# Priorities and PSUM banks in the tail of a four-layer convolution kernel: the last group's work against the third group's

## The chip, the cores and the metric

The kernel runs on one core of one Trainium2 chip. The metric is the device time of one execution in microseconds (us): the median of three runs. A profiled execution, taken apart from these, gives the trace; its times are counted from the start of its span. The engines are named as the profile has them: PE (matmuls), PEld (its weight loads), DVE (vector), ACT (activation), POOL, and SP (here only a queue that issues DMAs).

## The reference

The input x has shape (16, 32, 128, 128): 16 images of 32 channels. Four layers follow each other, each of the form x = x + layer(group_norm(x)) with 16 groups of two channels. The functions and the weights' names are the reference's, abridged:

```python
x = x + L0(gn(x), W2, b2, W1, b1)       # a recurrent layer that scans the diagonals of the image
x = x + L1(gn(x), weight)               # a 3x3 layer of sums of absolute differences, quantised
x = x + L2(gn(x), weights1)             # 2D Hartley transform, 32x32 low modes mixed, transformed back
x = x + L3(gn(x), conv1 .. conv7, deconv1 .. deconv3)

def L3(x):
    y = concatenate([norm(corr(x, op)) for op in five_edge_operators], axis=1)
    y = maxpool2(conv3x3(y, conv1))     # 160 -> 32 channels
    y = maxpool2(conv3x3(y, conv2))
    y = maxpool2(conv3x3(y, conv3))
    y = conv3x3(y, conv4)
    y = conv3x3(deconv2x2(y, deconv1), conv5)
    y = conv3x3(deconv2x2(y, deconv2), conv6)
    y = conv3x3(deconv2x2(y, deconv3), conv7)
    return x * y
```

The edge operators are linear and their norms need only a mean and a variance, so an edge operator, its norm and conv1 are together one 5x5 convolution of the image with weights that depend on the image's statistics.

## The kernel before, in words

The 16 images are worked as four groups of four images. Layer 0 runs first, on its own. Then `rest` (L498) does layers 1 to 3. Its class `Differences` makes layer 1 for all images with DVE (L760) and ACT (L757), summed on PE (L647). Its class `After` makes layers 2 and 3 of one group after the other. `After.work` is a Python generator: each step records a few instructions and yields how long they take or what is to be waited for. A `Weave` holds such a generator, a time `now` and a list of steps that are put off until later.

While layer 1 is being recorded, `Differences.run` draws steps of groups 0 to 2 from the first weave between its own, and `keep_order` (L471) then fixes that order on every engine. What is left of the third group (its last 5x5 chunk and all that follows) and the whole last group are recorded by `drain` (L455): of the two weaves it always takes the one whose `now` is smaller. When one of them has ended, the other gets `alone` = True.

This last part, the tail, has no order fixed by hand. The scheduler that lays out the program takes, among the instructions that its own estimate holds for ready, the one with the smallest priority number. The number is `tc.cur_priority` at the time of recording and counts up with each instruction, so that in the kernel before the order of recording decides. A queue, once laid out, is worked in its order on each engine, and SP's DMA issues are such a queue too.

The steps of one group that matter, with the lines that the profile shows:

- Layer 2, `forward`: images are loaded (`xh`, L1056), scaled by `scaling` (L1155 to L1170, with the matmuls L786, L795 and L1165), and transformed on PE by `first` (L1107), `turned` (L1122) and `second` (L1079), with DVE in between (L1111, L1067, L1070, L1083). The modes go to DRAM (`xm`, L1089) and come back (L1183); DVE adds mirrored modes (L1190, L1197). `mixing` multiplies with the weights `mix` (loads L1205, matmuls L1218), and the result goes through DRAM (L1242, L1273).
- Layer 2, `back`: the inverse transform in two steps. L1292 makes `o1` in two halves of four accumulators each, emptied by DVE (L1304). L1342 makes 16 pieces of two accumulators each; `take_out` adds a piece to the image on DVE (L1317) and takes its statistics (L1320). L1359, L786, L795 and small DVE steps up to L1361 make mean and scale.
- Layer 3, first part: ACT normalises the image (L1382), `statistics` sums products of shifted rows into four accumulators `gram` on PE (L1488), DVE reduces them with tables (L1557), and the weights of the 5x5 layer are made (L1625, L1627).
- Layer 3, `conv1` (the 5x5 layer): edge sums first (L1844), copied by L1856, then eight chunks of 16 rows. A chunk is 25 taps of 16 matmuls (L1871) into four accumulators of 128x512 fp32; edges are mended by L1888. At its end DVE adds the cut columns (L1905) and pools (L1764), and ACT or DVE adds the bias (L1789, L1786).
- Layer 3, the rest: conv2, conv3 and conv4 (L1661), then three upsampling steps of `Composed.round` (L908, with bias matmuls L934), the third of which is `last`, eight rounds of 128 L908 and 32 L934; each is multiplied into the residual by DVE (L1993), finished by ACT (L1958) and stored (L1967).

The last group is worked by `end`, a shallow copy of `after` with larger buffers, its image kept whole in SBUF (`whole`), and a PSUM pool of its own. The pool `b_ps` (`bg`) has four banks and serves groups 0 to 2; `c_ps` has the other four and serves the last group. `acc` (L995) hands out one bank: before the change, while `alone` is true every other four of the last group's accumulators come from `bg`, which is its `spare`; otherwise all come from its own pool. An accumulator can only be given out when what read the bank's previous content is done.

Of the kernel before, what the change touches and what calls it, by code (L numbers as in the profile page):

```python
# [350 lines left out]
class Weave:  # L351
# [59 lines left out]
    def step(self):  # L411
# [3 lines left out]
        if v is None:  # L415
            return None
        if v is SUMMED:
            wait = self.lag()
# [33 lines left out]
                self.pe = start + us * CLOCK  # L452


def drain(*weaves):  # L455

    live = list(weaves)
    for w in live:
        w.draining, w.stretch = True, 1.5
    while live:  # L460
        w = min(live, key=lambda w: w.now)
        us = w.step()
        w.now = max(w.now + (us or 0.0), w.until)
        w.due(float("inf") if us is None else w.now)
        if us is None:
            live.remove(w)
            for w in live:
                w.alone, w.stretch = True, 1.0


def keep_order(nc, tc, start):  # L471

    last = {}
    for i in nc.cur_bb.bb.instructions[start:]:
        if i.engine in last:
            tc.add_manual_dep(
                i,
                last[i.engine].name,
                mybir.DependencyInfo(mybir.DependencyClass.NoSync, mybir.DependencyReason.DATA),
                reason="order",  # L480
            )
        last[i.engine] = i
# [5 lines left out]
LATE, ACT_SPARE = 1.5, 1.5  # L488
SLACK, CLOCK = 1.0, 1.0
SUMMED = ("summed",)  # L490


def rest(nc, tc, cst, sel16, bias, m1, r1, a, d, out):


    with ExitStack() as ctx:
        sm = ctx.enter_context(tc.tile_pool(name="s1_sm", bufs=1))
        stat = sm.tile([128, B, 8, 6], F32, name="stat2")  # L498
        with tc.tile_pool(name="s1_ps0", bufs=2, space=PSUM) as ps:
            first = Differences(nc, sm, ps, cst, sel16, m1, r1, a["adder_w"], d, stat)  # L500
        bg = ctx.enter_context(tc.tile_pool(name="b_ps", bufs=4, space=PSUM))
        after = After(nc, tc, "left", sm, bg, cst, bias, a, d, stat, out)
        weave = after.weave = Weave(after.work(range(NG - 1)))
        start = len(nc.cur_bb.bb.instructions)
        with ExitStack() as front:
            first.run(tc, front, weave)
        keep_order(nc, tc, start)

        end = copy.copy(after)
        end.side, end.ps = "right", ctx.enter_context(tc.tile_pool(name="c_ps", bufs=4, space=PSUM))  # L510
        end.spare, end.whole = bg, True

        end.buffers = {"t_x": 8, "xm": 8, "xw": 4, "t_w": 6, "t_r": 8, "frames": 3, "gm": 5, "e_v": 6, "l_x": 4}
        end.weave = Weave(end.work([NG - 1]))
        end.weave.now = end.weave.base = weave.now
        end.weave.finished = B - 1
        drain(weave, end.weave)


class Differences:  # L520
# [259 lines left out]
def normalised(nc, pool, ps, weave, mv, n, avg, eps, out):  # L780
# [5 lines left out]
    nc.tensor.matmul(p[:, :n], avg, mean, start=True, stop=True)  # L786
    yield SUMMED
    nc.vector.tensor_copy(out[:, 0], p[:, :n])
# [6 lines left out]
    nc.tensor.matmul(p[:, :n], avg, v, start=True, stop=True)  # L795
    yield SUMMED
    nc.vector.tensor_copy(v, p[:, :n])
# [35 lines left out]
class Composed:  # L833
# [10 lines left out]
    def compose(self, pool, ps):  # L844
# [5 lines left out]
        for par in range(4):  # L850
            for tap in range(4):
# [6 lines left out]
                for i, (q, k) in enumerate(terms):  # L858
# [8 lines left out]
                    yield 0.4  # L867
        yield SUMMED
        t = pool.tile([128, 25, 32], F32, name="co_t")
# [9 lines left out]
        nc.vector.tensor_reduce(t[:, 24], w3.rearrange("p t o -> p o t"), AX.X, ALU.add)  # L879
        yield SUMMED  # L880
        nc.sync.dma_start(self.store, t.rearrange("p t o -> p (t o)"))
        p = ps.tile([128, 512], F32, name="acc")
        for j in range(4):
            nc.tensor.matmul(p[32 * j : 32 * j + 32, :1], t[:32, 24], self.bd[:32], start=True, stop=True)
        yield SUMMED
        nc.vector.tensor_add(self.bias, p[:, :1], self.b3)
# [76 lines left out]
class After:  # L963


    def __init__(self, nc, tc, side, sm, ps, cst, bias, a, d, stat, out):
        self.nc, self.tc, self.side, self.ps, self.cst, self.bias = nc, tc, side, ps, cst, bias
        self.a, self.d, self.stat, self.out = a, d, stat, out
        self.spare, self.banks, self.whole = None, 0, False
        self.sm, self.scales = sm, {}  # L970
        self.buffers = {"t_x": 4, "xm": 3, "xw": 2, "t_w": 3, "t_r": 4, "frames": 2, "gm": 3, "e_v": 3, "l_x": 2}
        store = [d["up"][i] for i in range(3)]
        self.up5 = Composed(nc, sm, a, "deconv1", "conv5", bias[:, 7:8], bias[:, 4:5], store[0])
        self.up6 = Composed(nc, sm, a, "deconv2", "conv6", bias[:, 8:9], bias[:, 5:6], store[1])
        self.up7 = Composed(nc, sm, a, "deconv3", "conv7", bias[:, 9:10], bias[:, 6:7], store[2])
# [19 lines left out]
    def acc(self):  # L995

        self.banks += 1
        ps = self.spare if self.weave.alone and self.banks // 4 % 2 else self.ps
        return ps.tile([128, 512], F32, name="acc")

    def prepare(self):
# [812 lines left out]
    def conv1(self, g, pool, frames, y1, sides, wf, b1):  # L1814

        nc, tc, cst, weave = self.nc, self.tc, self.cst, self.weave

        def tap_of(n, i):

            at, const = PART_AT[n]  # L1820
            size = PARTS[n][4] * PARTS[n][5]
            return wf[:, const if i == size else at + i, :]

        _, _, _, again, _, window = frames
# [33 lines left out]

        spreads = []
        for ch in range(8):  # L1860
            xp = window(ch)

            acc = [self.acc() for _ in range(4)]
            apart, at = (32, 4 * ch) if self.whole else (8, 0)
            edge = {0: ("t", 0, 0, 1), 7: ("b", 3, 3 * W, at + 3 * apart + 5)}.get(ch)
            for tap in range(25):
                kh, kw = tap // 5, tap % 5
                for j in range(4):
                    for blk in range(4):
                        rows = slice(32 * blk, 32 * blk + 32)  # L1870
                        nc.tensor.matmul(  # L1871
                            acc[blk][32 * j : 32 * j + 32, :],
                            tap_of("all", tap)[rows],
                            xp[rows, at + apart * j + kh : at + apart * j + kh + 4, kw : kw + W],
                            start=tap == 0,
                            stop=tap == 24,
                        )
                if edge and tap == 23:
                    n, j, first, row = edge
                    for part, col, wide in ((n, 0, 5), (n + "l", 1, 2), (n + "r", W + 1, 2)):  # L1880
                        width = W if wide == 5 else 1
                        o = first + (W - 1 if part == n + "r" else 0)
                        for cut_tap in range(2 * wide + 1):
                            for blk in range(4):
                                rows = slice(32 * blk, 32 * blk + 32)
                                c = col + cut_tap % wide
                                src = xp[rows, row + cut_tap // wide, c : c + width]
                                nc.tensor.matmul(  # L1888
                                    acc[blk][32 * j : 32 * j + 32, o : o + width],
                                    tap_of(part, cut_tap)[rows],  # L1890
                                    cst["ones"][rows, :width] if cut_tap == 2 * wide else src,
                                    start=False,
                                    stop=False,
                                    skip_group_check=True,
                                )
                            yield 0.1
                yield 1.06
            yield SUMMED
            if ch + ahead < 8:
                again(ch + ahead)  # L1900
            out = []
            for blk in range(4):
                sides_of = acc[blk].rearrange("p (r w) -> p r w", w=W)[:, :, :: W - 1]
                both = cut[:, blk, :, 4 * ch : 4 * ch + 4].rearrange("p s r -> p r s")
                nc.vector.tensor_tensor(sides_of, sides_of, both, ALU.add)  # L1905
                weave.dve += 0.17
                out.append(self.pooled(pool, acc[blk], 4, W))

            def spread(ch=ch, out=out):
                for blk in range(4):  # L1910
                    self.evict(
                        y1[:, blk, 1 + 2 * ch : 3 + 2 * ch, 1:65], out[blk], b1[:, blk : blk + 1], blk, nc.scalar
                    )
                if ch in (0, 7):
                    self.neighbours(y1, 16, ch == 7, ch == 0)

            spreads.append(weave.later(5.0, spread))
            yield -2.0
# [248 lines left out]
```

## Time and profile before

| what | us |
|---|---|
| median of 3 runs | 6466.08 |
| lowest and highest run | 6465.73, 6471.06 |
| profiled execution, its own time | 6473.52 |
| its span | 6471.7 |
| PE, DVE, ACT busy over the span | 5326.5, 5455.2, 5276.5 |
| last layer-1 instruction on DVE (L630) ends | 5632.5 |
| third group's last 5x5 chunk ends on PE | 5677.5 |
| last group's mixing (L1218) starts, ends | 5753.1, 5787.4 |
| its first and last take-out (L1317, L1320) | 5869.5, 5921.7 |
| its Gram matmuls (L1488) end | 6033.2 |
| its edge sums (L1844) start | 6067.2 |
| its 5x5 layer (L1871) starts, ends | 6087.3, 6302.5 |

The page shows busy time in 40 slices of 161.8 us each; the tail begins in slice 35. The stage views of the profile give, for each stretch of time, the busy time of each engine with the count of records, the mean granted PE clock (1.00 is full), and the share of the DMA engines. A timeline row is a start, a duration, an engine, a line, an operation, tiles, shapes and a count; in brackets stand the idle time ahead of it and what ended it. The chain of waits goes back from the last instruction to what released it at each step; "issue" is time in which PE waited for nothing that the profile shows.

### The profile page before, as it was taken

The numbers are of one execution on the slowest core, as the hardware profiler recorded it, in microseconds if no ns is written. First come the engines' busy times: TensorE is split into PE (matmuls) and PEld (weight loads), VectorE is DVE, ScalarE is ACT, GpSimd is POOL, SyncE is SP. The second block draws the span as 40 slices with busy tenths as digits, with TensorE's granted clock in tenths as the row PEclk, the third lists the DMA queues.
The fourth block names the chain that finished last, engine by engine and source line by source line (L and its number), as shares of the span: only waits on it lengthen the run. The fifth ranks groups of instructions, "written<-read, shape, count | busy, mean of one in ns | idle before, by whom it ended". The sixth has DMA issues, their size and how long they took to land.

```text
span 6471.7 us, 275922 instructions
## 1 busy us (share of the span) xinstructions
PE 5326.5 (82%) x130160; PEld 2805.8 (43%) x130160; DVE 5455.2 (84%) x6528; ACT 5276.5 (82%) x2779; POOL 58.7 (1%) x67
## 2 busy tenths in 40 slices
PE   3689577788877879998877879998888699977696
PEld 3576233344434433334443433334344333345594
DVE  7899899999999989999999889999999899834212
ACT  3899799999999989999999879999999899702001
POOL 0000000000000000000000000000000000000000
PEclk9999899999999989999999989999999899977898
DMA  7643313121154633222455532323455522344102
GB/s 313 222 178 125 87 48 84 48 57 45 32 138 124 204 117 88 64 72 73 142 147 150 168 93 58 97 51 102 129 144 179 162 58 63 97 131 137 33 4 65
DMA packets 363701, 700.94 MB, mean 108 GB/s; under 512 B 67972, under 2 KB 216452, under 8 KB 351684
## 3 DMA queue, kind: packets, MB, share of 16 engines
q1 hardware_dynamic: 355092, 648.86, 33.6%
q0 software_dynamic: 7040, 33.80, 1.6%
q8 instruction: 1018, 16.68, 1.1%
q14 instruction: 119, 0.97, 0.1%
q10 hardware_dynamic: 432, 0.64, 0.0%
HBM read 500.46 MB, written 182.69 MB: 106 GB/s over the span
## 4 chain that ended last, share of the span: by engine, by line
PE 26%; issue 11%; DVE 8%; ACT 3%; DMA 2%; SPq 0%; POOL 0%; DVEq 0%; ACTq 0%; POOLq 0%
PE acc L1871 10%; PE acc L647 9%; DVE d_dve L760 4%; PE acc L908 3%; ACT d_act L757 2%; PE acc L1661 1%; PE acc L1488 1%; PE acc L1292 1%; DMA xm_d<-xm 0%; PE acc L1218 0%; PE acc L662 0%; DVE pooled L1764 0%; PE acc L934 0%; DMA v<-fold_d 0%; PE acc L1844 0%
## 5 line engine op out<-in xcount | busy, mean ns | idle before, releaser
L757 ACT ACTIVATE d_act<-q,neg 128x8192 f16<-128x8192 f16 (+1 forms) x630 | 4463.6, 7152 | 215.9 <-PE acc L647 197.4
L760 DVE TENSOR_SCALAR d_dve<-q,qw 128x8192 f16<-128x8192 f16 (+1 forms) x1674 | 3868.3, 2360 | 215.3 <-PE acc L647 193.1
L647 PE MATMUL acc<-d_dve,sel 128*32 128x512 f16 x26784 | 1850.6, 395 | 409.4 <-DVE d_dve L760 305.6
L647 PEld LDWEIGHTS <-sel 128*32 128x32 f16 x36864 | 983.9, 99 | 1934.0 <-issue 1265.0
L647 PE MATMUL acc<-d_act,sel 128*32 128x512 f16 x10080 | 708.5, 401 | 147.9 <-ACT d_act L757 140.8
L1871 PE MATMUL acc<-xp,wf 32*32 32x512 f32 x19200 | 725.4, 607 | 23.0 <-issue 21.5
L677 PE MATMUL acc<-q,zero 128*32 128x512 f16 x8396 | 576.7, 390 | 7.1 <-issue 7.0
L223 PE MATMUL pg<-h,wb 64*64 64x20 f32 (+15 forms) x8192 | 341.3, 304 | 61.6 <-DVE h L251 34.8
L908 PE MATMUL acc<-y,u_conv 32*32 32x256 f32 x10752 | 318.4, 435 | 60.7 <-issue 45.1
L237 ACT ACTIVATE gt<-pg,bias 128x20 f32<-128x20 f32 (+15 forms) x1024 | 331.5, 383 | 41.6 <-PE pg L223 39.7
L1871 PEld LDWEIGHTS acc<-xp,wf 32*32 32x32 f32 x19200 | 222.4, 103 | 329.2 <-issue 297.9
L677 PEld LDWEIGHTS <-zero 128*32 128x32 f16 x8396 | 243.6, 99 | 228.1 <-issue 40.6
L1789 ACT ACTIVATE y<-pooled,b 128x128 f32<-128x128 f32 x112 | 39.5, 395 | 368.3 <-DVE pooled L1764 235.0
L223 PEld LDWEIGHTS pg<-h,wb 64*64 64x64 f32 x8192 | 251.4, 150 | 136.4 <-DVE h L251 81.5
L908 PEld LDWEIGHTS acc<-y,u_conv 32*32 32x32 f32 x10752 | 157.0, 110 | 164.3 <-issue 122.8
L1871 PE MATMUL acc<-image,wf 32*32 32x512 f32 x6400 | 207.8, 605 | 0.1
L223 PE MATMUL pg<-xn,wb 64*64 64x2 f32 (+63 forms) x4096 | 184.5, 290 | 25.9 <-issue 17.9
L1871 PEld LDWEIGHTS acc<-image,wf 32*32 32x32 f32 x6400 | 184.8, 103 | 20.3 <-issue 4.6
L1488 PE MATMUL acc<-xp 32*64 32x204 f32 (+2 forms) x6432 | 174.2, 338 | 15.8 <-issue 15.8
L1905 DVE TENSOR_TENSOR acc<-acc,cut 128x8 f32<-128x8 f32 x128 | 19.4, 166 | 193.4 <-PE acc L1871 193.1
L1661 PE MATMUL acc<-y,w_conv 32*32 32x512 f32 (+2 forms) x4608 | 144.3, 481 | 30.3 <-issue 18.0
L662 PE MATMUL acc<-q,sel 32*32 32x512 f16 x4608 | 158.4, 393 | 4.0 <-issue 4.0
(242 smaller groups left out, 3725.9 us busy)
## 6 DMA issues: line engine op xcount, KB each, us to landing
q<-q_d SPq DMA_DIRECT2D x128, 536.2 KB, 10.2
xp<-xn_d SPq DMA_DIRECT2D x24, 2112.0 KB, 9.1
x_in<-in_x_dram SPq DMA_DIRECT2D x16, 2048.0 KB, 14.7
xn<-in_xs_dram SPq DMA_DIRECT2D x64, 512.0 KB, 7.0
res<-in_x_dram SPq DMA_DIRECT2D x64, 512.0 KB, 8.9
x_d<-res SPq DMA_DIRECT2D x64, 512.0 KB, 4.6
xq<-x_d SPq DMA_DIRECT2D x256, 128.0 KB, 4.4
xr<-x_d SPq DMA_DIRECT2D x256, 128.0 KB, 4.3
```

Source lines behind the costliest of these rows:

```text
L223: nc.tensor.matmul(bank[c][q][64 * pair : 64 * pair + 64, :, :width], wb[half, 4 * kind + KIND[q]].rearrange("p b o -> p (b o)"), v[half], ...
L237: nc.scalar.activation(gt[:, q, :, :n], bank[c][q][:, :, :n], AF.Tanh if q == G else AF.Sigmoid, bias=bias[:, KIND[q] : KIND[q] + 1],)
L647: self.nc.tensor.matmul(acc[k][32 * j : 32 * j + 32, :], self.sel16[:, i // 9, :], d[:, row : row + 4, c : c + W], start=first, stop=last,)
L662: self.nc.tensor.matmul(acc[k][32 * j : 32 * j + 32, :], self.sel16[rows, 8, :], q[rows, row : row + 4, kw : kw + W], start=False, stop=False,
L677: self.nc.tensor.matmul(acc[k][32 * j : 32 * j + 32, :], self.zero, q[:, :4, :W], start=False, stop=False)
L757: nc.scalar.activation(dst, src, AF.Relu, bias=self.neg[:, i : i + 1])
L760: nc.vector.tensor_scalar(dst, src, self.qw[:, i : i + 1], 0.0, ALU.subtract, ALU.max)
L908: nc.tensor.matmul(acc[blk][32 * j : 32 * j + 32, o : o + rows * n], t[part, 4 * par + tap, :], own[:, top : top + rows, left : left + n], ...
L1292: nc.tensor.matmul(pa[blk][32 * r : 32 * r + 32, 32 * o : 32 * o + 32], zi[part, 16 * oh + o, :], cst["cas_t"][part, 32 * r : 32 * r + 32] ...
L1488: nc.tensor.matmul(gram[blk][j : j + width, at : at + n], xp[part, l, 2 + j : 2 + j + width], xp[part, rows, j : j + width + 4], start=sta ...
L1661: nc.tensor.matmul(acc[blk][32 * j : 32 * j + 32, : rows * n], wc[name][part, tap, :], pick(part, blk, j)[:, tap // 3 : tap // 3 + rows, t ...
L1871: nc.tensor.matmul(acc[blk][32 * j : 32 * j + 32, :], tap_of("all", tap)[rows], xp[rows, at + apart * j + kh : at + apart * j + kh + 4, kw ...
```

## The change

`drain` gets the tile context. It gives each of the two weaves a count of priorities of its own: the third group's starts at the current number plus 2,000,000, the last group's at plus 1,000,000. Before each step it sets `tc.cur_priority` to that weave's number and keeps it afterwards. Which weave records next is decided as before, so the instructions and their order of recording are the same. The bank rule in `acc` changes: `spare` is used when `self.late` is true, in place of when the weave is alone; `late` is set False in `__init__`, and at each chunk of `conv1` to whether the chunk is the fifth or a later one. `alone` still decides how DVE and ACT share `evict` and `spread`. Below `BEHIND` all line numbers grow by four.

```diff
-def drain(*weaves):
+def drain(tc, *weaves):
 
     live = list(weaves)
+    turn = {w: tc.cur_priority + BEHIND * (len(live) - k) for k, w in enumerate(live)}
     for w in live:
         w.draining, w.stretch = True, 1.5
     while live:
         w = min(live, key=lambda w: w.now)
+        tc.cur_priority = turn[w]
         us = w.step()
         w.now = max(w.now + (us or 0.0), w.until)
         w.due(float("inf") if us is None else w.now)
+        turn[w] = tc.cur_priority
         if us is None:
             live.remove(w)
...
+BEHIND = 1000000
...
-        drain(weave, end.weave)
+        drain(tc, weave, end.weave)
...
-        self.spare, self.banks, self.whole = None, 0, False
+        self.spare, self.banks, self.whole, self.late = None, 0, False, False
...
-        ps = self.spare if self.weave.alone and self.banks // 4 % 2 else self.ps
+        ps = self.spare if self.spare and self.late and self.banks // 4 % 2 else self.ps
...
-            xp = window(ch)
+            xp, self.late = window(ch), ch >= 4
```

## Prediction

> **What bounds the kernel now.** I read the page's slices first: until slice 35 DVE, ACT and PE are full; from about 5629 us of the span on, only the tail (third group's end and the whole last group) runs. I then took that tail stage by stage (busy time by stage), because the change touches nothing earlier.
>
> ```profile
> core 0: us, PE busy (x) PEld busy (x) DVE busy (x) ACT busy (x) POOL busy (x), PEclk, DMA share, GB/s
> 5753.00:5788.00 35.00, 20.91 (x1247) 17.36 (x1245) 8.98 (x19) 0.00 (x0) 0.00 (x0) 0.55 0.20 65
> 5788.00:5870.00 82.00, 50.52 (x2339) 35.80 (x2317) 17.08 (x36) 2.55 (x4) 0.00 (x0) 0.62 0.63 177
> 5870.00:5922.00 52.00, 47.29 (x1122) 34.18 (x1109) 46.26 (x77) 8.59 (x8) 0.00 (x0) 0.70 0.39 124
> 5922.00:5937.00 15.00, 11.08 (x382) 7.43 (x366) 7.51 (x31) 0.39 (x1) 0.07 (x1) 0.89 0.41 152
> 5937.00:6034.00 97.00, 75.17 (x2952) 57.83 (x2940) 15.52 (x59) 30.39 (x58) 3.06 (x6) 0.93 0.28 93
> 6034.00:6067.00 33.00, 0.99 (x4) 0.93 (x4) 30.45 (x78) 0.00 (x0) 2.16 (x4) 0.51 0.24 90
> 6087.00:6303.00 216.00, 215.13 (x6794) 192.47 (x6801) 26.62 (x83) 6.05 (x15) 0.00 (x0) 0.99 0.02 4
> ```
>
> The end is set by the last group's chain: mixing (L1218, to 5787), inverse transform (L1292), 16 take-outs on DVE (L1317, L1320; 5870 to 5922, DVE 46 of 52 us), statistics, normalising on ACT and Gram matmuls (L1488, to 6033), a DVE chain with PE empty (to 6067), edge sums (L1844), then the 5x5 layer (L1871) on a full PE for 216 us. Third-group work (L1661, L908, L934, L1993) shares the queues until 5985.
>
> The chain that ended last shows a second limit, where matmuls are small: work, then "issue".
>
> ```profile
> 6067.93 1.88 PE acc L1844 x115
> 6069.81 2.23 issue
> 6072.04 1.53 PE acc L1844 x82
> 6073.58 2.21 issue
> ```
>
> ```profile
> q8 instruction: 1018, 16.68, 1.1%
> ```
>
> By packets and MB, a packet of the instruction queue is 16.4 KB, and the L1844 steps repeat every 3.75 us. The records hold an fp32 matmul twice (12,800 of the 5x5 layers are 25,600 records), and L1488 steps are 128 records in 3.5 to 3.75 us: PE takes small matmuls at about 57 ns each whatever the clock. One round of the third group's last layer (128 L908 and 32 L934) took 9.4 us (5917.8 to 5927.2).
>
> The third view is the timeline at the first chunk boundary of the last 5x5 layer.
>
> ```profile
> 6117.68 32.91 PE L1871 MATMUL acc<-image,wf 32*32 32x512 f32 x995
> 6118.90 0.26 DVE L1905 TENSOR_TENSOR acc<-acc,cut 128x8 f32<-128x8 f32 x2 [31.11 <-PE acc L1871]
> 6119.11 1.29 DVE L1764 TENSOR_REDUCE pooled<-acc 128x128 f32<-128x512 f32 x2
> 6120.32 0.24 DVE L1905 TENSOR_TENSOR acc<-acc,cut 128x8 f32<-128x8 f32 x2
> 6120.52 1.29 DVE L1764 TENSOR_REDUCE pooled<-acc 128x128 f32<-128x512 f32 x2
> ```
>
> PE goes straight on at 6117.68 because the next chunk has other banks; DVE has emptied the old four only at 6121.81.
>
> [...] L788, which the last group's statistics wait for, ran at 5929.94, behind four third-group L1993 (5927.29, 2.73 us). [...]
>
> **The change, part by part.** *Order.* In the changed program's built order every engine has the same instructions; only places differ, on PE from the third group's last 5x5 chunk to the last L908. On PE all third-group work still stands ahead of L1844: the 5x5 layer does not overlap with it, and only waits before L1844 can be won. POOL is unchanged. On SP two of the third group's last stores go behind four w_conv loads, on ACT its last eight L1958 behind all L1382: neither is waited for before 6080, so I cost them at nothing.
>
> *Banks.* `end` is a copy of `after`, made when the third group is past its chunk 4, so it inherits late=True. The build confirms it: half of the last group's accumulators lie in the third group's banks (0 to 3) from its first transforms on; and its chunks 0 to 3 of the 5x5 layer, which before alternated between sets, all lie in 7, 4, 5, 6. So it is not what the words say.
>
> My walk goes through the new order with the old durations (times of the span, before -> after):
> - Last third-group chunk. L786, L795 and three L1107 now stand ahead of some 450 of its matmuls. The xh loads land 10.4 us after issue, from 5643.7 on, 3.3 us apart; PE waits for three of them and for DVE, about 12 us, of which I take 4 as fetch stalls that it had anyway (3.1 us at 5653.65). End 5677.5 -> 5685.5.
> - Forward transforms. All of conv2's first half (144 L1661 by 73 ns, 10.5 us) and a bank wait of 5.5 now precede the second L1122; then 10 us of transforms, 11.4 of conv2, 11.5 of transforms: last L1083 5728.7 -> 5735.
> - SP's queue keeps its order but for six mix loads in one piece; they wait for the last L1107 (about 5731, were 5719). The last xm store follows them (5741.4 -> 5749), and L1218 came 11.7 us after it; conv3, conv4 and a round (some 22+8 us from 5735) also stand ahead on PE: start 5753.1 -> 5765. L1218 is now unbroken: 512 by 57 ns, 29 us, where it took 34: end 5787.4 -> 5794.
> - L1292 starts 11 us later, 5805. Before, 689 instructions took 53.2 us to its end; now 889 stand there, since its two borrowed banks per half wait for third-group rounds: 200 by 58 ns, 11.6 us, and 4 us of bank waits. With two L1304: first take-out 5869.5 -> 5877. This includes a gain: 14 us before the first take-out (o1 was ready at 5855.4) go.
> - Take-outs. Eight use own banks: 8 by 2.4 us, 19. The other eight need a third-group round's banks, and PE and DVE alternate: rest of a round 8, L1993 3, two take-outs 5, L1993 and wait 1.5, round 8.5, L1993 2.5, four take-outs with waits 11, L1993 1, round 7.5, L1993 2.5: 70 us to L1359 instead of 52: 5921.8 -> 5947.
> - Statistics. L1359 to L1361 lose the 4.3 us PE wait, the L1993 and a wait: 14.8 -> 7.5, so ACT starts 5936.6 -> 5954.5.
> - Gram. Two of four accumulators are borrowed: 536 L1488 (30.3 us, from 2 us on), 60 instructions of a round (3.5), L1993 (3.2), round (9.2), L1993 (3.2), round (9.2), two L1993 (1.9), 536 L1488 (30.3), less 3 for instructions fetched during the waits: 89.8, where it was 96.6. End 6033.2 -> 6044.3.
> - DVE to L1844: 18 of 20 L1557 still follow, with two L1993 in place of the two: 34 us as before. L1844 6067.2 -> 6078.5, about 11 later.
> - 5x5 layer. Chunks 1, 2, 3 wait until DVE has emptied the four banks: 6121.8+0.1 less 6117.7, 4.2 us each, less 2, 11 and 2 matmuls of chunk 4 (66 ns) put there: 4.1+3.5+4.1. Chunk 4's fourth block waits for one bank, 0.7; chunk 0 for L1856, 0.7. Sum 13.1. Nothing covers these: no third-group work is left.
> - After it, order and alternation are as before: nothing.
>
> Sum: 11.3+13.1 = 24.4. The profiled execution took 6473.5 (span 6471.7 and 1.8 around), 7.4 over the median of 6466.1; the tail is the same in both, so the change is set on the median: 6466.1+24.4 = 6490.5; I say 6490.
>
> Bounds of what the trace doesn't show: the borrowed-bank coupling, from 46 us of take-outs (16 by 2.4 and 11 L1993 by 0.67, DVE alone) to 78 with half-clock rounds; the forward part, from 5 us earlier (no xh wait matters) to 12 later; the chunk waits 10 to 15.
>
> **Rivals.**
> - *The sharing is hidden (not slower).* Priority gains count in full, if PE finishes each round under DVE's take-outs. Then take-outs are 46, the Gram's two L1993 waits go (6.4): 24.4-24-6.4 = -6, 6460. Decides from a round under 5 us, for then DVE never waits. For it: 43 ns per L908 at full clock; against: 9.4 us per round measured and blocks of instructions that set it.
> - *Only the chunk waits count.* Losses and gains before L1844 cancel: +13, 6479. For it: the place of L1844 in PE's queue is unchanged, and 25 us of waits are truly removed (14+7+4 of L1958 in ACT). Against: 18 us in the take-outs.
> - *Clock and fetch make it worse.* [...] With the upper bounds: take-outs 8 more, forward part 5, chunks 2, two Gram rounds of 11.5 instead of 9.2, 5: 20 more, 6510.
> - *It acts as its words say.* Then the last group would wait for no third-group bank before chunk 4; the built banks exclude it.
>
> **How the numbers follow.** Forecast 0.5 (6482 to 6500), only chunk waits 0.18, worse 0.15, hidden 0.17 with 0.07 of it beyond -0.2%. 0.2% is 13 us, about what a measurement of this kernel can tell from no change. Slower (over 6479): 0.5+0.15+half of 0.18 = 0.74; same: the other 0.09 and 0.10 of hidden, 0.19; faster 0.07. The range goes from 6464 to 6510: below it lie about 0.08 of hidden, above it half of the worse case.
>
> **What would show it.** Right: gaps of about 4 us on PE at three boundaries of L1871 on `image`; L1359 near 5947; L1218 in one piece; L1488 in two halves with L908 between. Wrong: L1844 starting before 6065, or no gaps at the boundaries.

## The result, and the profile after

| | before | after |
|---|---|---|
| median of the timed runs, us | 6465.9 | 6604.49 |
| lowest and highest | 6465.63, 6471.06 | 6595.52, 6614.80 |
| profiled execution, its span | 6473.52, 6471.7 | 6595.52, 6593.7 |

The ratio is 1.0214, with a 95% interval of 1.0201 to 1.0228: slower by about 138 us, where 24 were forecast. Below `BEHIND`, L1488 of before is L1492 after, L1871 is L1875, L908 is L912, L1993 is L1997.

The stage view of the changed kernel, cut at the points that the prediction names (busy us and, in brackets, records of PE, PEld, DVE, ACT and POOL; then granted clock, DMA share, GB/s):

```profile
core 0: us, PE busy (x) PEld busy (x) DVE busy (x) ACT busy (x) POOL busy (x), PEclk, DMA share, GB/s
5748.00:5777.00 29.00, 15.57 (x1044) 14.81 (x1047) 5.59 (x12) 0.00 (x0) 0.00 (x0) 0.50 0.23 77
5777.00:5857.00 80.00, 51.19 (x2102) 35.08 (x2104) 17.48 (x35) 2.54 (x4) 0.00 (x0) 0.59 0.66 181
5857.00:5930.00 73.00, 69.83 (x1223) 52.12 (x1222) 47.16 (x77) 7.87 (x8) 0.00 (x0) 0.62 0.25 79
5938.00:6028.00 90.00, 87.45 (x1093) 62.77 (x1105) 6.93 (x45) 22.14 (x50) 3.13 (x6) 0.50 0.16 66
6028.00:6055.00 27.00, 21.42 (x760) 14.30 (x728) 6.68 (x13) 4.29 (x4) 0.00 (x0) 0.81 0.28 81
6055.00:6144.00 89.00, 88.41 (x1080) 84.40 (x1088) 2.51 (x4) 0.00 (x0) 0.00 (x0) 0.50 0.01 2
6144.00:6179.00 35.00, 18.46 (x356) 12.76 (x352) 31.18 (x78) 2.32 (x2) 2.15 (x4) 0.50 0.33 116
6199.00:6425.00 226.00, 223.31 (x6768) 171.79 (x6768) 24.70 (x76) 5.64 (x14) 0.00 (x0) 0.99 0.02 4
```

The rows 5938 to 6028 and 6055 to 6144 are the two halves of the Gram products, two blocks in each, with third-group rounds between them. This order was forecast. Their lengths were not: 90 and 89 us, on a PE that is busy all the time, for some 1080 records each. The kernel before did 1717 records, all but a few of them of the same line, in 51 us (its stage row):

```profile
5982.00:6033.00 51.00, 40.14 (x1717) 35.79 (x1711) 2.73 (x4) 4.30 (x4) 0.00 (x0) 1.00 0.16 45
```

A matmul of the program is two records, so that is 59 ns per matmul there and 165 ns here, at a granted clock of 1.00 there and 0.50 here. The view of one line's instructions (duration in ns, least, median, most; then what the idle time ahead of them ended with) says the same, before and after:

```profile
L1488 PEld LDWEIGHTS acc<-image x2144: 100/132/227, 5939.6 to 6033.0; 32*64 32x64 f32 x184, 32*32 32x32 f32 x11
L1488 PE MATMUL acc<-image x2144: 187/331/598, 5939.6 to 6033.0; 32*64 32x204 f32 x181, 32*32 32x36 f32 x7, 32*32 32x72 f32 x4, 32*64 32x68 f32 x2
its engine sat idle before it (us, times) until:
  issue: 30.3, 37
```

```profile
L1492 PEld LDWEIGHTS acc<-image x2144: 120/225/226, 5940.9 to 6143.7; 32*64 32x64 f32 x182, 32*32 32x32 f32 x13
L1492 PE MATMUL acc<-image x2144: 248/542/597, 5940.9 to 6143.7; 32*64 32x204 f32 x180, 32*32 32x72 f32 x7, 32*32 32x36 f32 x6, 32*64 32x68 f32 x1
its engine sat idle before it (us, times) until:
  ACT image L1394: 6.0, 2
  DVE xr L1997: 2.2, 2
  issue: 2.1, 6
```

Before, 30.3 us of PE's idle time in this line are "issue", and PE goes in steps: in its timeline, from 5999.32 to 6028.73, 128 records take about 3.02 us and the next 128 start 3.5 to 4.0 us after them. In the 51 us of the stage row above, 13 packets of the instruction queue (q8) came, one in 3.9 us. From this the author takes it that the fetching of instructions set the pace there; no view names it, and the 4 and 3 us that the prediction puts down to fetching are its estimates. After, "issue" is 2.1 us, q8 brings 9 packets in each half, one in 10 us, and PE is busy for 87.45 of 90 and 88.41 of 89 us. Its waits for others are 8 us in all, so the 115 us are not a wait.

The chain that ended last, at the chunk boundaries of the changed kernel's last 5x5 layer:

```profile
6232.54 27.89 PE acc L1875 x762
6260.43 0.24 DVE acc L1909 x2
6260.67 0.02 issue
6260.69 0.70 DVE pooled L1768
6261.39 0.14 issue
6261.52 27.89 PE acc L1875 x729
```

The boundary waits are there too: DVE (L1909, L1768) now stands on the path, 1.1 us ahead of a chunk's first matmul. The chain shows only the first of the four banks. The weight loads just behind it, from the timeline, go to one block at a time as DVE empties the other three:

```profile
6261.49 0.13 PEld L1875 LDWEIGHTS acc<-image,wf 32*32 32x32 f32 x2 [1.14 <-PE acc L1875]
6262.09 0.14 PEld L1875 LDWEIGHTS acc<-image,wf 32*32 32x32 f32 x2 [0.46 <-issue]
6262.90 0.14 PEld L1875 LDWEIGHTS acc<-image,wf 32*32 32x32 f32 x2 [0.67 <-issue]
6263.50 0.58 PEld L1875 LDWEIGHTS acc<-image,wf 32*32 32x32 f32 x33 [0.46 <-issue]
```

Between the starts of PE's records, gaps of more than 0.25 us come to 2.5, 2.5 and 3.3 us at the first three boundaries and to 1.6 us at the fourth.

To set the walk of the prediction beside the trace, times have to be counted from a common point: the last of SP's `x_d<-xr` issues (L340) starts at 5632.1 before and at 5619.0 after, with the same instructions ahead of it. Shifts below are those of the span plus 13.1.

| point | before | after | shift | forecast |
|---|---|---|---|---|
| third group's last chunk ends | 5677.6 | 5668.2 | +3.7 | +8 |
| L1218 starts | 5753.1 | 5748.3 | +8.3 | +12 |
| L1218 ends | 5787.4 | 5777.0 | +2.7 | +7 |
| L1359 starts | 5921.8 | 5929.7 | +21.0 | +25 |
| L1361 ends | 5936.6 | 5937.9 | +14.4 | +18 |
| Gram products end | 6033.2 | 6144.0 | **+123.9** | **+11** |
| edge sums (L1844) start | 6067.2 | 6179.0 | +124.9 | +11 |
| end of the span | 6471.7 | 6593.7 | +135.1 | +24 |

### The profile page after: what moved, and what is told of

It is laid out like the page before. It is cut to its first block, busy times and chain, and to the rows that moved or that the text cites. A ratio compares the mean times of both kernels' runs of the same rounds, so it can differ in the third digit from the quotient of the medians.

```text
span 6593.7 us, 275909 instructions
## 1 busy us (share of the span) xinstructions
PE 5487.8 (83%) x130160; PEld 2917.4 (44%) x130160; DVE 5453.4 (83%) x6528; ACT 5277.1 (80%) x2779; POOL 58.7 (1%) x67
## 4 chain that ended last, share of the span: by engine, by line
PE 41%; issue 26%; DVE 19%; ACT 10%; DMA 3%; SPq 1%; POOL 0%; DVEq 0%; ACTq 0%; POOLq 0%
PE acc L651 13%; PE acc L1875 13%; DVE d_dve L764 11%; ACT d_act L761 6%; PE acc L912 3%; PE pg L223 3%; PE acc L1492 3%; PE acc L1665 2%; ACT gt L237 2%; ACT junk L198 1%; DVE stat L124 1%; PE acc L1296 1%; PE acc L666 1%; DMA xq<-x_d 1%; DMA x_in<-in_x_dram 1%
## 5 line engine op out<-in xcount | busy, mean ns | idle before, releaser
L1875 PE MATMUL acc<-xp,wf 32*32 32x512 f32 x19200 | 723.8, 606 | 19.6 <-issue 19.6
L912 PE MATMUL acc<-y,u_conv 32*32 32x256 f32 x10752 | 345.6, 447 | 55.3 <-issue 42.3
L1875 PEld LDWEIGHTS acc<-xp,wf 32*32 32x32 f32 x19200 | 222.0, 103 | 322.0 <-issue 291.8
L1962 ACT ACTIVATE xr<-xr,stats 128x1024 f32<-128x1024 f32 x48 | 52.1, 1149 | 310.3 <-DVE xr L1997 310.2
L912 PEld LDWEIGHTS acc<-y,u_conv 32*32 32x32 f32 x10752 | 171.7, 113 | 166.8 <-issue 124.0
L1875 PE MATMUL acc<-image,wf 32*32 32x512 f32 x6400 | 218.2, 605 | 3.0 <-DVE pooled L1768 1.8
L1909 DVE TENSOR_TENSOR acc<-acc,cut 128x8 f32<-128x8 f32 x128 | 19.5, 166 | 233.6 <-PE acc L1875 233.4
L1492 PE MATMUL acc<-xp 32*64 32x204 f32 (+2 forms) x6432 | 175.9, 340 | 15.8 <-issue 15.8
L1875 PEld LDWEIGHTS acc<-image,wf 32*32 32x32 f32 x6400 | 164.3, 103 | 54.1 <-issue 12.7
L1561 DVE CUSTOM_DVE_ANT_0 es_w<-acc,gm 128x420 f32<-128x420 f32 x80 | 47.6, 595 | 159.4 <-PE acc L1492 152.2
```

Source lines behind the costliest of these rows:

```text
L912: nc.tensor.matmul(acc[blk][32 * j : 32 * j + 32, o : o + rows * n], t[part, 4 * par + tap, :], own[:, top : top + rows, left : left + n], ...
L1492: nc.tensor.matmul(gram[blk][j : j + width, at : at + n], xp[part, l, 2 + j : 2 + j + width], xp[part, rows, j : j + width + 4], start=sta ...
L1875: nc.tensor.matmul(acc[blk][32 * j : 32 * j + 32, :], tap_of("all", tap)[rows], xp[rows, at + apart * j + kh : at + apart * j + kh + 4, kw ...
```

## The experiments

First question: why do the Gram products of two blocks take 165 ns each? Theories: A, two blocks use only two of the array's four row groups (32 of 128 rows each); B, two PSUM banks limit; C, the clock comes from the surroundings; D, PE waits for other work. Second: what do the two parts of the change, and its words, give by themselves? Each ratio is of the means of all executions, against the kernel before on the same chip.

| run | us | before | ratio (95%) |
|---|---|---|---|
| e1 Gram in own banks | 6488.4 | 6459.3 | 1.0041 (1.0028 to 1.0053) |
| e2 two passes by blocks | 6568.0 | 6459.3 | 1.0148 (1.0113 to 1.0183) |
| e3 two passes by columns | 6485.6 | 6459.3 | 1.0041 (1.0026 to 1.0056) |
| e4 as e2, four banks | 6571.6 | 6459.3 | 1.0170 (1.0148 to 1.0191) |
| e5 flag off | 6593.2 | 6463.3 | 1.0199 (1.0184 to 1.0214) |
| e6 priority alone | 6511.8 | 6463.3 | 1.0070 (1.0055 to 1.0085) |
| e7 bank rule alone | 6480.7 | 6463.3 | 1.0028 (1.0019 to 1.0038) |
| e8 flag from first chunk | 6589.2 | 6463.3 | 1.0190 (1.0175 to 1.0205) |
| e9 counts start equal | 8464.7 | 6462.3 | 1.3100 (1.3078 to 1.3122) |
| e10 third group 400 ahead | 8110.1 | 6462.3 | 1.2550 (1.2532 to 1.2569) |
| e11 three blocks, then one | 6536.5 | 6462.3 | 1.0115 (1.0100 to 1.0130) |
| e12 recorded 40 us earlier | 6472.4 | 6467.2 | 1.0004 (0.9998 to 1.0011) |
| e13 as e2, a spare matmul | 6568.2 | 6465.4 | 1.0134 (1.0073 to 1.0195) |
| e14 as e2, two spare ones | 6563.2 | 6465.4 | 1.0147 (1.0126 to 1.0168) |
| e15 e2 again | 6579.6 | 6465.4 | 1.0177 (1.0161 to 1.0192) |
| e16 four blocks, then two | 6479.7 | 6459.3 | 1.0027 (1.0019 to 1.0035) |

**e1, on the changed kernel.**

```diff
-        gram = [self.acc() for _ in range(4)]
+        self.banks += 4
+        gram = [self.ps.tile([128, 512], F32, name="acc") for _ in range(4)]
```

> The changed kernel, but the four Gram accumulators come from the last group's own pool, so all four blocks can be worked in one stretch. Theory A (row groups: with two blocks at a time the products use only 64 of the array's 128 rows): the Gram matmuls become one stretch of about 60 us at a clock near 1 instead of 86.8 + 88.4 us at 0.50, and the time falls by about 114 us, 6480 to 6495. Theory B (two PSUM banks limit the writes): the same here. Theory C (the half clock comes from what lies around this stage, not from the split): the stretch stays at 0.50 and over 150 us, the time over 6580. Theory D (PE waits for the normalising or for third-group rounds): the stretch is as long as what it waits for, time over 6570.

Its stages, Gram first, then the third-group rounds that used to lie between the halves:

```profile
5944.00:6007.00 63.00, 50.72 (x2166) 43.98 (x2175) 5.99 (x41) 19.21 (x44) 0.48 (x1) 0.97 0.20 77
6007.00:6046.00 39.00, 32.54 (x1112) 22.21 (x1086) 19.67 (x52) 4.29 (x4) 0.00 (x0) 0.78 0.19 57
```

All 1072 matmuls take 63 us. The loss falls from 138 to about 26 us (0.41%). D is out, and so is C as the whole cause (e16 comes back to what lies ahead of the stage). What is left has the forecast's size: in its trace L1844 starts 10.4 us late and the end comes 20.4 us late, counted as above. That it also comes so near the forecast's 11 and 24 is partly luck, for the way there is another: the Gram products end 17 us earlier than before, and 61.6 us lie between their end and L1844 instead of 34, with third-group rounds in between.

**e2, e3, e4: the kernel before, with the last group's Gram products made in two passes.** The first pass runs inside the loop (`both(xp, ch, l)` makes the products of one row), the second after it, held behind the first on PE's queue.

```diff
+                    if self.whole and blk // 2 != turn:      # e2, e4
+                    if self.whole and j // 64 != turn:       # e3
+                        continue
...
-                        gram[blk][j : j + width, at : at + n],
+                        gram[2 * (blk % 2) + (j // 64 + turn) % 2 if self.whole else blk][j : j + width, at : at + n],   # e4
...
+            for ch in range(H // 16):                    # after the loop: the second pass
+                xp = chunk(ch)
+                for l in range(2, 18):
...
+                    both(xp, ch, l, 1)
...
```

> The kernel before, all banks as they were, only the last group's Gram products recorded in two passes: blocks 0 and 1 for all rows, then blocks 2 and 3. Same matmuls, same third-group work around them. Theory A: 162 ns per matmul instead of 60: 1072 of them take about 175 us where they took 64, granted clock 0.50, time 6466 + 108 = about 6575 (6560 to 6590). Theory B: the same. Theories C and D: no change beyond 10 us, 6460 to 6476.

> The kernel before with two passes again, but split by the half of the output columns (0 to 63, then 64 to 127), so each pass uses all four row groups and all four banks, and only half the array's columns. Theory A: about 60 ns per matmul, time within 15 us of 6466. Theory B: within 15 us of 6466 too. A wider form of A (half of the array is at work, whichever half): as slow as the split by blocks, about 6575 at clock 0.50.

> The kernel before in two passes by blocks (0 and 1, then 2 and 3), but each half of a block's output columns goes to a bank of its own, so each pass writes four banks from two row groups. It leaves out that the sums of one block stay in one bank: halves of two blocks share a bank, so the statistics mix blocks. Theory A: as slow as the two passes with two banks, about 6575 at clock 0.50. Theory B: about 60 ns per matmul, within 15 us of 6466.

The stretch with nothing but Gram products on PE, in e2, then e3, then e4:

```profile
5975.00:6131.00 156.00, 156.00 (x1894) 112.29 (x1888) 3.52 (x8) 4.30 (x4) 0.00 (x0) 0.50 0.05 15
```

```profile
5971.00:6050.00 79.00, 79.00 (x1881) 69.39 (x1876) 2.34 (x4) 4.29 (x4) 0.00 (x0) 1.00 0.10 30
```

```profile
5991.00:6147.00 156.00, 156.00 (x1896) 112.10 (x1896) 1.94 (x3) 4.30 (x4) 0.00 (x0) 0.50 0.05 15
```

e2 makes the loss in the kernel before, without any of the change: 165 ns per matmul at 0.50. e4 has the same pace with four banks: B is out. e3, with all rows and half the columns, has 84 ns at 1.00: with half of the array a matmul takes 84 ns instead of 59, and the halved clock makes the rest. That also corrects theory A, which had put e3 at 60 ns. In e3, as in e2, four tiles of 32x64 are at work. If they work side by side, which the author assumes, one matmul keeps its tile for 4 times 84, 336 ns, at full clock, and for 4 times 165, 660 ns, at half. This is an estimate from the pace, and not the duration of a record (331 and 542 ns, median). By the same estimate eight tiles would come to 42 ns, less than the 59 ns at which their matmuls came before; four come to more.

**e11: three blocks, then one** (`blk // 3 != turn` in e2).

> The kernel before with the last group's Gram products in two passes by blocks, now three blocks (0, 1, 2) and then the fourth alone. From the runs so far: two row groups cost 163 ns per matmul at clock 0.50; in the 5x5 layer of the kernel with the flag off, three blocks ran at 72 ns at clock 1.00 and one block alone at 428 ns at 0.50, four at 64 ns. Theory A (the array's rows decide, and the clock falls to half below three row groups): the three-block pass keeps the clock at 1.00 and about 60 ns; the lone block takes twice the two-block price, 326 ns at 0.50: 268 matmuls, 87 us where they took 16, so 6466 + 70 = about 6535 (6525 to 6550). Rival A2 (any pass with less than the whole array falls to half clock): three blocks at about 109 ns, 0.50; 6466 + 110 = 6575.

```profile
5990.00:6023.00 33.00, 31.91 (x1087) 30.82 (x1073) 0.00 (x0) 0.40 (x1) 0.00 (x0) 1.00 0.18 53
6032.00:6106.00 74.00, 74.00 (x438) 51.64 (x434) 0.00 (x0) 0.00 (x0) 0.00 (x0) 0.50 0.00 1
```

61 ns with three row groups at full clock, 338 ns with one at half (two tiles, so 676 ns for a matmul and tile); the time was met within 2 us. The granted clock is still 1.00 up to 6023, with three blocks, and 0.50 from 6032 on, with the fourth alone. A2 is out.

**e13, e14, e15: is it the amount of work?** To e2's passes, matmuls on the idle row groups are added, whose results nobody reads; e15 is e2 unchanged.

```diff
+                for blk in (2 - 2 * turn,) if self.whole else ():      # e14: also 3 - 2 * turn
+                    part = slice(32 * blk, 32 * blk + 32)
+                    nc.tensor.matmul(
+                        gram[blk][j : j + width, GRAM : GRAM + width + 4],
+                        xp[part, l, 2 + j : 2 + j + width],
+                        xp[part, rows.start, j : j + width + 4],
...
```

> The kernel before with the Gram products in two passes by blocks, and after each pair of matmuls of a pass one spare matmul on a third row group, a third as long (68 columns instead of 204), into unused columns of an accumulator. It adds 536 matmuls whose results nobody reads. Theory A3 (of the 163 ns, a factor of two is the granted clock, and the clock follows how much of the array is at work): the spare work lifts the clock to 1.00, and the pass falls to 83 ns per useful matmul or what 1608 matmuls of 59 ns need, 89 to 100 us for 1072 where the two passes alone took 175: 6485 to 6505. Rival (the clock stays at half, the spare matmuls only lie beside): 6570 to 6590.

> As before it, with one such spare matmul on each of the two idle row groups: 1072 added. Theory A3: clock 1.00, bounded by the fetching of 2144 matmuls of 59 ns, 127 us: about 6525 (6515 to 6540). Rival (half clock): 6570 or more.

> The two passes by blocks once more, unchanged. Of its ten timed executions eight took 6555 to 6580 us and two 6487 to 6491. If two row groups lie near the point at which the clock is halved, some executions keep 1.00 and take what the split by columns took, about 6486, and others about 6568, and nothing between. If those two were of another cause, all are near 6568 here.

e13, then e14:

```profile
5986.00:6133.00 147.00, 147.00 (x2674) 127.47 (x2670) 0.00 (x0) 0.00 (x0) 0.00 (x0) 0.50 0.04 11
```

```profile
5986.00:6120.00 134.00, 134.00 (x3250) 120.31 (x3248) 0.00 (x0) 0.00 (x0) 0.00 (x0) 0.50 0.01 3
```

A3 fell: the clock stays at 0.50. A third of e13's records are spare, so 891 useful matmuls took 147 us; half of e14's are, 812 in 134 us: 165 ns in both, as in e2, so the spare ones lie beside for nothing. Still, one of e13's four executions took 6488.5 us and two of e2's ten 6486.6 and 6491.1, while all four of e15 took 6572 to 6585. A level of 80 us less and nothing between is near what full clock in this stage would give, by an estimate from e2's 165 ns and e3's 84: 1072 matmuls by 81 ns, 87 us. The granted clock of whole executions, which was kept for each, fits: 0.927 to 0.933 in these three, 0.916 to 0.922 in the other fifteen of e2, e13 and e15. There is no trace of any of the three.

**e16: enter the two-block part at full clock.** The first half of the rows has all four blocks in one pass; only the second half is split as in e2. Against e2:

```diff
-                    if self.whole and blk // 2 != turn:
+                    if self.whole and turn < 2 and blk // 2 != turn:
...
-                both(xp, ch, l)
+                both(xp, ch, l, 0 if ch >= 4 else 2)      # 2: all four blocks
...
-            for ch in range(H // 16):
+            for ch in range(4, H // 16):
```

> The kernel before, with the Gram products of the first half of the image's rows in one pass of all four blocks, and only the second half in two passes by blocks. When the two-block passes begin, PE has run some 19 us of four-block work without a wait, at clock 1.00. If a clock once at full is kept by two row groups (the clock remembers what lay before, theory H): 536 matmuls of 83 ns instead of 59, 13 us more, 6475 to 6490. If two row groups bring it to half whatever lay before (theory R): 536 of 163 ns, 56 us more, 6515 to 6530, with a record at 1.00 that ends within a few us of the change to two blocks.

Four blocks, then two:

```profile
5990.00:5999.00 9.00, 7.55 (x320) 6.77 (x307) 0.00 (x0) 0.00 (x0) 0.00 (x0) 1.00 0.02 4
6002.00:6041.00 39.00, 39.00 (x930) 36.81 (x925) 1.21 (x4) 0.00 (x0) 0.00 (x0) 1.00 0.01 3
```

H holds: two blocks keep the full clock for the 39 us shown, with 84 ns per matmul as in e3, and the loss is 0.27%. So, over these 39 us, two row groups by themselves did not bring the clock down; in the changed kernel it was down before them, and they did not lift it. Its first half found the clock at half: the 8 us ahead of it, 5930 to 5938, have 0.50. Ahead of the second half PE is idle for 1.70 us ("issue") and 0.87 us (for L1997; timeline at 6053.92 and 6055.59), the record of half clock begins at 6055.2, and it lasts for 150.2 us, until the 5x5 layer with its four blocks has run for 6 us.

**e7, e6, e5, e8: the parts and the words.** e7 has the old `drain` with the new `acc`; e6 the new `drain` with the old `acc`; e5 and e8 are the changed kernel with the flag off on the last group's copy, e8 with it on again from the first chunk:

```diff
-        end.spare, end.whole = bg, True
+        end.spare, end.whole, end.late = bg, True, False
...
-            xp, self.late = window(ch), ch >= 4
+            xp, self.late = window(ch), True      # e8 alone
```

> The bank rule of the change (inherited flag and all) without its priorities. In the built order two blocks of the Gram products go first for 35 matmuls only, the other 1037 or so have all four. Theory A: Gram near 60 ns per matmul once all four blocks run, no stretch at 0.50 longer than some 10 us; what is left is the chunk waits (13 us) and bank waits before (about 10): 6480 to 6500. Rival (borrowed banks as such make the Gram slow): over 6560.

> The priorities of the change without its bank rule (the borrowed banks come when the weave is alone, as before). Third-group work is then built between the Gram products and the edge sums. Theory A: Gram one stretch of 60 us, clock near 1; some 60 us gained ahead of it, 125 to 150 us of third-group matmuls behind it of which the 34 us of DVE reduction and little else hide: 6500 to 6540. No chunk waits in the 5x5 layer. Rival (priority is what made the changed kernel slow, by half clock): Gram over 150 us, over 6580.

> The changed kernel with the flag set to False on the last group's copy, so that it does what the words of the change say: own banks until the fifth chunk of the 5x5 layer. In the built order the Gram products are then one stretch of all four blocks, and most of the third group (412 conv2 to conv4 matmuls and all rounds of its last upsampling) stands between chunks 3 and 4 of the last group's 5x5 layer. Theory A: Gram 60 us at full clock. What the tail gains ahead of the edge sums, by not waiting for third-group work (14 + 6 + 7 + 33 us): 60. What the third group's work costs where nothing else needs PE: about 125 us of matmuls and 3 us of DVE wait per round; chunk waits 12. 6466 - 60 + 150 = 6540 to 6570. If the third group's place did not matter (rival), about 6410 to 6440.

> The changed kernel with the flag False until the 5x5 layer and True from its first chunk on: priorities, unsplit Gram, no waits at chunk boundaries. In the built order three blocks of chunk 0 wait for the whole third group. Theory A: Gram 60 us at full clock; then the third group's 125 to 150 us stand exposed, less what chunk 0's and 1's own blocks cover (nothing, the queue is in order): 6466 - 60 + 150 = 6540 to 6560. If the third group's place does not matter (rival): 6400 to 6430.

e7 has its Gram products in four-block turns, with a granted clock of 0.87 over 5940 to 6045, and a 5x5 layer 10 us longer: the bank rule costs little where the scheduler does not put one half of the blocks behind the other. e6 brings the Gram products' end 117 us forward (from L340's issue on, 284.5 us instead of 401.1), but the third group's matmuls then take 182 us between the Gram products and DVE's last steps to the edge sums, with PE busy for 140 of the 180 us shown. Little of it is hidden: L1844 starts 54 us late.

```profile
5904.00:6084.00 180.00, 140.00 (x4552) 93.65 (x4529) 53.70 (x130) 15.43 (x16) 0.00 (x0) 0.76 0.27 89
```

e5 does what the words of the change say, and is as slow as the change. The edge sums start 115 us earlier, the third group costs 165 us behind chunk 3, and the built order has one block of chunk 4 by itself ahead of the third group and one of chunk 5 after it. Four blocks, the first lone block, then three blocks:

```profile
6024.00:6049.00 25.00, 25.00 (x781) 17.37 (x782) 0.86 (x3) 0.40 (x1) 0.00 (x0) 1.00 0.02 4
6084.00:6116.00 32.00, 32.00 (x152) 9.82 (x148) 0.00 (x0) 0.00 (x0) 0.00 (x0) 0.50 0.00 1
6124.00:6140.00 16.00, 16.00 (x461) 13.23 (x444) 0.00 (x0) 0.00 (x0) 0.00 (x0) 1.00 0.01 3
```

64 ns, 421 ns at half clock, 69 ns. At these paces two lone blocks of 100 matmuls cost 2 times 36 us, which is why e5 missed its expectation on the slow side. In e8 a block each of chunks 0 and 1 goes alone in the same way, and the time is as long (6589.2 us). It is the changed kernel's loss a second time, in another layer.

**e9, e10, e12: a version that beats both?** e6 gains 117 us ahead of the edge sums and pays more behind; a smaller lead might keep some of it. e9 is e6 with `BEHIND = 0`, e10 with `BEHIND = -400`.

> The priorities of the change, each weave with its own count, but both counts start at the same number (the lead of 1,000,000 becomes 0), and the bank rule of before. In the built order 1312 of the third group's last 1776 upsampling matmuls still stand behind the start of the Gram products, which they are mixed with, all four blocks in turn. Theory: against the version with full priority (6512) some 464 matmuls of 59 ns, 27 us, and the third group's conv2 to conv4, 42 us, come under the waits of the last group's chain, less 10 to 20 us that they disturb it: 6450 to 6475, so no clear gain on the kernel before. Rival (the waits of the third group's rounds for DVE hold up the Gram products in the queue): over 6480.

> As the version with both counts from the same number, but with the third group's count 400 ahead: 966 of its 1776 upsampling matmuls are behind the start of the Gram products, none behind their end. Theory: 20 us more of it is covered, but it stands ahead of the last group's transforms again: 6445 to 6475. Rival: the order of recording in the kernel before is already the best mix, 6466 to 6485.

Both are far off. e9 between 7000 and 7700 us:

```profile
7000.00:7700.00 700.00, 700.00 (x2142) 190.59 (x2142) 8.83 (x12) 8.80 (x8) 0.00 (x0) 0.50 0.04 13
```

With equal counts the scheduler takes mostly one matmul of each group in turn, L1492 on 32x64 tiles and L912 (or its bias matmul L938) on 32x32 tiles, and they take 654 ns each on average at 0.50 (700 us by 1071) instead of about 60. The author puts this down to the change of tile shape from one matmul to the next; a run that alternates within one tile shape was not made, so it is not shown. e12 shifts the order of recording by whole steps instead, in the kernel before:

```diff
-        end.weave.now = end.weave.base = weave.now
+        end.weave.now = end.weave.base = weave.now - 40.0
```

> The kernel before, only the last group's clock of recording starts 40 us earlier, so that in the order of recording it stands ahead of the third group by whole steps, and not by single matmuls; no priorities, banks as before. In the built order 816 of the third group's 1776 upsampling matmuls (336 before) stand behind the start of the Gram products, none behind their end, and both change turns in pieces of 8 to 64 matmuls. Theory (mixing single matmuls of two tile shapes cost the runs with equal priorities their 1650 to 2000 us, at about 0.6 us for each; pieces of 16 pay little of that): the last group's chain starts the Gram products earlier and PE does the rest beside ACT's normalising; 6440 to 6475. Rival (every change of turn costs as much as in those runs): about 100 changes more, 0.6 us each, 6510 or more.

No change in the time. In the trace L1361 ends 23 us earlier from L340's issue on, but the Gram products end 11 us later (411.9 us against 401.1): the third-group matmuls moved from ahead of the Gram products to among them. None of the runs beats the kernel before.

## Why the prediction was wrong

- *Sign and build.* Right. The copy inherits the flag, the borrowed banks couple the two groups, the Gram products come in two halves with rounds between.
- *Forward part, take-outs, statistics.* Right in kind and nearly in size: L1359 21 us late where 25 were forecast (the first take-out's L1320 only 0.5 us late where 7.5 were forecast for it, the 16 take-outs 20 us longer where 18 were), L1218 in one piece of 28.7 us for 29, the DVE stretch to L1844 35 us for 34.
- *5x5 layer.* Right in kind and near in size: 11.3 us longer where 13.1 were forecast (L1871 on `image` from its start on the chain to its last record: 213.7 us before, 225.0 after; its last record before ends at 6301.0; at 6302.5, given as its end in the table of the kernel before, conv2 is already at work). The gaps at the first three boundaries are 2.5 to 3.3 us, not about 4: PE begins with the first block when its bank is empty, and does not wait for all four.
- *The failed step is the term "536 L1488 (30.3 us" in the Gram sum, used twice.* It measured 86.8 and 88.4 us: 114.6 us more than the sum had, against 114 between the forecast and the measured median. That these agree to the microsecond is chance: other terms were up to 7 us off, and the profiled execution is 9 us below the median. The error stood one section earlier, "PE takes small matmuls at about 57 ns each whatever the clock". That pace was read from L1488 with four blocks at work at 1.00 (128 records in 3.5 to 3.75 us) and from the edge sums at 0.50 (6067 to 6087: 707 records in 20.00 us, 57 ns per matmul), and was carried to a stretch where only two blocks have a bank. e3 and e16 put the price of half the array at 84 ns, 27 us for 1072 matmuls; half the clock, 165 ns, is the other 87 us.
- *Could it have been seen blind?* Hardly. For the first part one might have divided a record of L1488 (331 ns) by the four tiles that two blocks leave, 83 ns, but that would have been luck: at half clock the same division gives 542/4 = 136 ns where 165 were measured. That the pace was 57 ns at 0.50 and at 1.00 said only that something other than the matmuls' own time set it, and not by how much. The second part could be seen only as a bound: the stages ahead were at 0.55 to 0.70.
- *The rivals.* "Clock and fetch make it worse" had the half clock as a cause, which in the Gram products is 87 us, but at the wrong place and, with 20 us, a fifth of the size: it priced the clock in take-outs and rounds, not in the Gram products. "It acts as its words say" was rightly excluded, and would have been as slow (e5).

## What to carry to other kernels

When small matmuls share the array, count the tiles that are at work in each stretch: the Gram products here took 59 ns with eight tiles and 61 with six (e11) at full clock, 84 with four at full clock, 165 with four and 338 with two at half: from four down, the time for which a matmul keeps its tile (an estimated 336 ns at full clock, 660 to 676 at half) divided by the tiles. A scheduler that waits for banks can take tiles away without any wait showing: PE was busy for 88.41 of 89 us. Look also at the clock at which a stretch begins: with half the rows at work, the second Gram half of the changed kernel, just after the PE waits of 1.70 and 0.87 us, was at 0.50 for its whole 89 us, and the two-block part of e16, behind four blocks at 1.00, was at 1.00 for 39 us. Before work of two groups is mixed by priority, look in the built order at what then stands next to what.

## What the runs showed of the hardware that was not expected

- In the changed kernel PE was busy for 88.41 of 89 us with two row groups at 0.50 throughout; in e2 and e4 it was busy for all of 156 us at 0.50. In e16 two row groups came behind four at 1.00 and were at 1.00 for the 39 us shown. Three row groups were at 1.00 (e11, 33 us, 61 ns; e5, 16 us, 69 ns). One was at 0.50 (e11, 74 us, from 9 us behind a stretch at 1.00 on; e5, 32 us).
- Spare matmuls of a third of the length on the idle row groups, in the profiled executions, neither raised the clock from 0.50 nor slowed the others from 165 ns (e13, e14). What the clock follows, if not the number of rows with full-length work, stays open.
- Single matmuls of 32x64 and 32x32 tiles in turn took 654 ns each on average at a granted clock of 0.50 (e9).
